# A selective-scan layer on Trainium2: gates made with the input projections and kept in DRAM, and the closing norm done in PSUM

## The chip, the cores and the metric

The kernel runs on one core of one Trainium2 chip. The metric is the device time of one execution in microseconds (us). The numbers are fp32 almost throughout, and one launch computes all four layers of the reference. The engines go by the names of the profile: PE (TensorE matmuls), PEld (its weight loads), DVE (VectorE), ACT (ScalarE), POOL (GpSimd) and SP (SyncE, which here issues the DMA transfers). Each engine takes its instructions strictly in the order in which the program lists them, and waits where an operand is not ready.

## The reference

The change lies in the first of four layers, a selective scan over 8 images of 64 channels and 64x64 pixels. Cut to what matters (L = 4096 pixels, DI = 128 inner channels, N = 16 states, K = 4 directions):

```
def _ss2d(x, ...):                                   # x: layer-normed input, B x H x W x 64
    xz = einsum('bhwc,dc->bhwd', x, in_proj_w) + in_proj_b
    xi, z = split(xz, 2, axis=-1)                    # z is the gate
    xc = silu(dwconv3(transpose(xi), conv_w, conv_b))
    xs = [xc by rows, xc by columns, both reversed]  # the 4 directions
    dts, Bs, Cs = split(einsum('bkdl,kcd->bkcl', xs, xproj_w), ...)
    dts = softplus(dtproj(dts) + dtproj_b)
    # the scan, per direction and state n:
    #   h = h * exp(dt * A) + dt * B * u ;  y += h * C
    y = sum over the directions (+ D * xs)
    y = _ln(y, outnorm_g, outnorm_b) * silu(z)       # norm and gate
    return einsum('bhwd,cd->bhwc', y, outproj_w) + outproj_b
xh = xh + _ss2d(_ln(xh, ln1_g, ln1_b), ...)
```

The other three layers (two attentions and a small trained modifier) are not touched.

## The kernel before

**Tiling and steps.** The scan layer is `scan_layer`. Channels DI lie on the 128 partitions. An image's 4096 pixels are cut into 4 chunks of 1024 (`CH`), and each of the 4 directions goes over the 4 chunks: 16 *steps* for each image, 128 in all. A step has 16 *units*, one for each state n. Below, "step 14, unit 6" means s = 14 and n = 6 of an image, both counted from 0, and images are counted from 0 to 7.

**A unit** (main loop, L991 to L1020, and `unit`, L800) has on each engine:

- ACT: `decay` (L762) makes a = exp(dt*A), issued two units ahead. For the four states in `BY_POOL` (0, 3, 6, 8), ACT copies the product that POOL made into the PSUM tile z (L777, in `spread`, at the top of the unit before). `save_state` (L798) copies one column.
- PE: for the other twelve states, PE spreads B into z (L780). Then `sum_up` (L882) adds up y = h*C over the states, in PSUM.
- DVE: z * (dt*u) (L807, twelve states) and the scan itself (L811), which gives h.
- POOL: `ct * h` (L816), and bt * (dt*u) for the four states (L770).
- SP: one load of `ct` (L758) per unit, a row of 1024 values spread to 128 partitions, 512 KB written, one unit ahead; four such loads of `bt` per step.

h and a have three buffers each, z two (PSUM), ct five.

**Background work.** Everything else is cut into *items*, a pair `(make, use)`, and put into the queue of `Background` (`bg`, L166). In each unit `bg.before` takes one item and runs its `make` (as a rule matmuls into one of two PSUM banks of 512 columns, `bank`), and at the end of the unit `bg.after` runs the `use` of the item taken the unit before (what ACT, DVE or SP do with the bank). `bg.later(f)` runs f in the same unit's `after`. The item `none` is an empty turn. In units 6, 7 and 8 (and 9 in some steps) no item with a `make` is taken. Convolutions are *groups* of up to 9 parts, at most one group a step (`credit`), which take turns with the items.

- `before(b)` (L494) makes the items for the input side of image b: load x (L507), layer norm (`norm_x`, L384: `centre` L392 to L398, `variance` L405, then a chain of small steps through DRAM for the inverse root, then `apply` L416 to L422), `project_in` (L513, L517), and eight `convolve` groups (nine matmuls L534, and Silu on ACT at L543).
- `after(b, ...)` (L564) makes the items for the output side: the squares of y (L446), `variance` (L451), the same chain, then per block of 512 pixels (eight for each image) `apply` (L470 spreads the inverse root with PE, L475 multiplies on DVE, L476 scales and shifts by on_g and on_b on ACT), `gate` (L578 projects the kept normed x with PE, L581 Silu on ACT, both issued in the same unit through `bg.later`; L589 multiplies on DVE) and `project_out` (L597, L598, L604, store L605).
- `inverse_root` (L350) holds the chain: store of the variances (L359), fetch (L366), square root on ACT (L369), reciprocal on DVE (L373), store (L374), fetch back (L378), with empty turns between.
- Silu and the square root need another function set on ACT than Exp and Ln: each of them has an ACT_TABLE_LOAD ahead of it, and `exp_and_ln` (L338) one behind it (L340).
- `pieces` (L692) splits B into three bf16 parts for a coming step: hooks at units 5, 7, 8, 9, 10 and 13 of the steps that need it. `rest(i)` puts matmuls on PE and, in the same hook, the copy of their result on ACT (L736).

**When things start.** At step 0, unit 4 of image b the items of `after(b - 1)` are queued; at step 1 of image b (step 4 of image 0) `start(b + 1)` queues those of `before(b + 1)`. In the steady images the blocks of the output side run in steps 2 to 4, the input norm in steps 5 to 7, `project_in` in 7 and 8, the convolutions from step 8 to step 0 of the next image. At the end of a unit's loop body:

```
if s == 0 and n == LAG + 2 and b > 0:
    last = images.pop(b - 1)
    bg.add(after(b - 1, last["row"], last["x"]))
    ...
if s == (1 if b else NCH) and n == 0 and b + 1 < NB:
    start(b + 1)
```

The last image's output side runs in pairs of blocks from step 13 on; the last pair comes after the scan, with nothing beside it.

Of the kernel before, what the change touches and what calls it, by code (L numbers as in the profile page):

```python
# [18 lines left out]
NB = 8  # L19
C = 64  # L20
# [224 lines left out]
def scan_layer(cm, x_in, w, xh):  # L245

    tc, nc = cm.tc, cm.nc
    with ExitStack() as ctx:
# [101 lines left out]
        def inverse_root(nb):  # L350
# [25 lines left out]
            def back(_):  # L376
                sm["r"] = work.tile([NBK, BK], F32, name="rstd", tag="rstd", bufs=1)[:nb]
                nc.sync.dma_start(sm["r"], rs.rearrange("(j f) -> j f", j=nb))  # L378

            chain = [none, (None, fetch), none, none, (None, root), (None, invert), none]  # L380
            chain += [(None, back), none, none]
            return put, chain, sm

        def norm_x(b, xn, pairs, project_in):  # L384
# [46 lines left out]
            out += chain  # L431
            out += [apply(i) for i in pairs[:2]] + [none] * (2 - len(pairs[:2]))
            for i in pairs:
                out += [project_in(2 * i), project_in(2 * i + 1)]
                if i + 2 in pairs:
                    out.insert(-1, apply(i + 2))
            return out

        def norm_y(y, blocks, load, gate, project_out):
# [25 lines left out]
            def apply(j):  # L465
# [7 lines left out]
                def use(ps):  # L473
                    v = y[:, bass.ts(j, BK)]
                    nc.vector.tensor_tensor(v, v, ps, ALU.mult)  # L475
                    nc.scalar.activation(v, v, AF.Identity, bias=on_b, scale=on_g)  # L476
# [6 lines left out]
            out += chain  # L483
            out += [apply(j) for j in blocks[:2]] + [gate(j0)]
            for j in blocks:
                if j + 2 in blocks:
                    out.append(apply(j + 2))
                out += [gate(j + 1) if j + 1 in blocks else none, project_out(j)]
            return out
# [3 lines left out]

        def before(b):  # L494

            xn = io.tile([2 * C, NBK // 2, BK], F32, name="xn", tag="xn")
# [4 lines left out]
            u = io.tile([DI, L], F32, name="u", tag="u")  # L501
            rows = BK // S
# [6 lines left out]
            def project_in(j):  # L509
# [6 lines left out]
                def use(ps):  # L516
# [3 lines left out]
                    )  # L520

# [37 lines left out]
            items = [[(None, load(j)) for j in range(NBK)]]  # L559
            for pairs in FIRST if b == 0 else (range(NBK // 2),):  # L560
                items.append(norm_x(b, xn, pairs, project_in))
            return u, block, items, [convolve(j) for j in range(NBK)]

        def after(b, y, block, blocks=range(NBK)):  # L564
# [4 lines left out]
            def load(j):  # L569
                xr = work.tile([C, BK], F32, name="xr", tag="xr", bufs=3)  # L570
                nc.sync.dma_start(xr, xf[:, bass.ts(j, BK)])
                gated[j] = xr

            def gate(j):
                def make():
                    ps = bank("zps")
# [1613 lines left out]
```

## Time and profile before

| what | number |
|---|---|
| runs | 12229.28 us median of 3 (12226.62 to 12230.54) |
| the profiled execution | 12228.28 us |
| its span, first to last instruction | 12226.5 us |
| scan layer, first to last scan instruction (L811) | 91.2 to 6913.5 us |
| start of images 1 to 7 (first scan of each) | 1002.3, 1841.4, 2681.0, 3522.7, 4364.5, 5203.5, 6053.0 us |
| DVE busy, whole span | 10380.4 us, 85% |
| ACT busy, whole span | 7575.7 us, 62% |
| POOL busy, whole span | 7247.3 us, 59% |
| PE busy, whole span | 11196.6 us, 92% |

The views used are: the page with the busy share of each engine in 40 equal slices of the span; the groups of instructions (line, engine, operation, out<-in, shapes, count, then busy us and mean ns of one, then the idle time just ahead of them and what ended most of it); the windows (busy us and number of instructions of PE, PEld, DVE, ACT and POOL in a stretch, then granted clock, DMA share and GB/s); and the timeline (start us, length, engine, line, operation, out<-in, and in brackets idle time before it and what ended that). "Idle" of an engine in a stretch is its length less the busy time. In the windows an instruction that overlaps the next is not counted twice. The scan layer fills the first 57% of the span, the first 23 slices.

### The profile page before, as it was taken

The numbers are of one execution on the slowest core, as the hardware profiler recorded it, in microseconds if no ns is written. First come the engines' busy times: TensorE is split into PE (matmuls) and PEld (weight loads), VectorE is DVE, ScalarE is ACT, GpSimd is POOL, SyncE is SP. The second block draws the span as 40 slices with busy tenths as digits, with TensorE's granted clock in tenths as the row PEclk, the third lists the DMA queues.
The fourth block names the chain that finished last, engine by engine and source line by source line (L and its number), as shares of the span: only waits on it lengthen the run. The fifth ranks groups of instructions, "written<-read, shape, count | busy, mean of one in ns | idle before, by whom it ended". The sixth has DMA issues, their size and how long they took to land. (4 is left out here: it accounts for less than half of the span.)

```text
span 12226.5 us, 120204 instructions
## 1 busy us (share of the span) xinstructions
PE 11196.6 (92%) x39087; PEld 4103.2 (34%) x39087; DVE 10380.4 (85%) x7400; ACT 7575.7 (62%) x10304; POOL 7247.3 (59%) x3326
## 2 busy tenths in 40 slices
PE   7899999999999999999998799999987779999999
PEld 2233333333333333333322233232335463333333
DVE  4999999999999999999999776868778676676767
ACT  4666667766667676676675554645547574555554
POOL 4999999999999999999999500000007480000000
PEclk8999999999999999999999899999998779999999
DMA  3666666666666666666666400000011100000000
GB/s 112 205 210 217 210 211 214 212 212 210 213 212 207 210 216 209 212 213 211 205 203 211 135 20 25 6 25 8 17 49 34 41 20 24 19 4 19 5 11 6
DMA packets 522899, 1528.62 MB, mean 125 GB/s; under 512 B 125312, under 2 KB 142352, under 8 KB 519696
## 3 DMA queue, kind: packets, MB, share of 16 engines
q1 hardware_dynamic: 522256, 1520.80, 37.9%
q8 instruction: 312, 5.11, 0.2%
q14 instruction: 331, 2.71, 0.1%
HBM read 1439.63 MB, written 72.09 MB: 124 GB/s over the span
## 5 line engine op out<-in xcount | busy, mean ns | idle before, releaser
L816 POOL TENSOR_TENSOR ct<-ct,h 128x1024 f32<-128x1024 f32 x2048 | 4789.4, 2362 | 296.8 <-DVE h L811 133.1
L882 PE MATMUL yps<-ct,lno_cen 128*128 128x512 f32 x8192 | 4119.9, 633 | 58.6 <-ACT yps L869 57.2
L811 DVE TENSOR_TENSOR_SCAN h<-a,state,z 128x1024 f32<-128x1024 f32 x1536 | 3570.4, 2341 | 82.5 <-ACT z L777 39.7
L762 ACT ACTIVATE a<-dt,amat 128x1024 f32<-128x1024 f32 x2048 | 2347.1, 1147 | 1134.8 <-DVE h L811 1128.1
L1191 DVE TENSOR_TENSOR sum<-sum,ex 128x1024 f32<-128x1024 f32 x1920 | 2347.5, 1223 | 618.5 <-ACT ex L1184 483.1
L1184 ACT ACTIVATE ex<-sc 128x1024 f32<-128x1024 f32 x2048 | 1968.0, 1024 | 1359.6 <-PE sc L1179 1359.2
L882 PEld LDWEIGHTS yps<-ct,lno_cen 128*128 128x128 f32 x8192 | 1476.4, 195 | 2078.9 <-issue 1818.0
L807 DVE TENSOR_TENSOR z<-z,e 128x1024 f32<-128x1024 f32 x1536 | 1859.8, 1211 | 128.0 <-PE z L780 75.5
L1198 PE MATMUL av<-ex,v 128*64 128x512 f32 x8192 | 1950.0, 604 | 0.0
L1179 PE MATMUL sc<-q,k 16*128 16x512 f32 (+1 forms) x8192 | 1562.1, 623 | 4.2 <-ACT q L1172 3.1
L780 PE MATMUL z<-bs,pick 48*128 48x512 bf16 x3072 | 941.9, 387 | 388.4 <-DVE h L811 339.5
L811 DVE TENSOR_TENSOR_SCAN h<-a,z 128x1024 f32<-128x1024 f32 x512 | 1161.3, 2281 | 75.0 <-ACT z L777 59.8
L770 POOL TENSOR_TENSOR bt<-bt,e 128x1024 f32<-128x1024 f32 x512 | 1209.8, 2363 | 5.4 <-DMA bt<-bc 5.4
L1505 POOL TENSOR_TENSOR gt<-gt,pad 128x1024 f32<-128x1024 f32 x16 | 34.9, 2179 | 1575.0 <-ACT gt L1504 1575.0
L1198 PEld LDWEIGHTS av<-ex,v 128*64 128x64 f32 x8192 | 512.2, 136 | 1332.7 <-issue 1278.9
L1179 PEld LDWEIGHTS sc<-q,k 16*128 16x128 f32 (+1 forms) x8192 | 528.2, 184 | 1016.4 <-issue 977.4
L777 ACT COPY z<-bt 128x1024 f32<-128x1024 f32 x512 | 519.9, 1015 | 406.0 <-DVE h L811 309.2
L780 PEld LDWEIGHTS <-pick 48*128 48x128 bf16 x3072 | 175.9, 95 | 1514.5 <-DVE h L811 931.4
L534 PE MATMUL vps<-pad,convd 128*128 128x512 f32 x1152 | 573.8, 599 | 0.1
L1878 DVE RECIPROCAL r<-e 128x512 f32<-128x512 f32 x128 | 420.6, 3322 | 0.0
L1881 POOL TENSOR_TENSOR r<-r,half 128x512 f32<-128x512 f32 x128 | 162.7, 1271 | 361.9 <-issue 186.0
L798 ACT COPY state<-h 128x1 f32<-128x1 f32 x2048 | 362.9, 177 | 0.0
(417 smaller groups left out, 9594.8 us busy)
## 6 DMA issues: line engine op xcount, KB each, us to landing
ct<-bc SPq DMA_DIRECT2D x2048, 512.0 KB
bt<-bc SPq DMA_DIRECT2D x512, 512.0 KB
x<-x SPq DMA_DIRECT2D x12, 2048.0 KB
bc<-e SPq DMA_DIRECT2D x128, 128.0 KB
x<-x SPq DMA_DIRECT2D x32, 512.0 KB
part<-x SPq DMA_DIRECT2D x128, 128.0 KB
bsd<-bp SPq DMA_DIRECT2D x192, 64.0 KB
bs<-bsd SPq DMA_DIRECT2D x128, 96.0 KB
```

The source lines that it names most:

```text
L534: nc.tensor.matmul(held[0].rearrange("p (r c) -> p r c", c=S), convd[:, t, :], pad[:, j * rows + dy : (j + 1) * rows + dy, dx : dx + S], s ...
L762: ctl["exp", n] = nc.scalar.activation(ctl["a", n], ctl["dt"], AF.Exp, scale=amat[:, ctl["k"], n : n + 1])
L770: nc.gpsimd.tensor_tensor(bt, bt, ctl["dus"], ALU.mult)
L780: nc.tensor.matmul(z[:, bass.ts(i, BK)], pick[:, n : n + 1].to_broadcast([3 * N, DI]), ctl["bs"][:, bass.ts(i, BK)], start=True, stop=True,)
L807: first = nc.vector.tensor_tensor(z, z, ctl["dus"], ALU.mult)
L811: nc.vector.tensor_tensor_scan(h[:, flip], a[:, flip], z[:, flip], 0.0 if state is None else state[:, n : n + 1], ALU.mult, ALU.add,)
L816: freed[at] = nc.gpsimd.tensor_tensor(ct, ct, h, ALU.mult)
L882: nc.tensor.matmul(ctl["ps"][:, bass.ts(i, BK)], lno_cen, ct[:, bass.ts(i, BK)], start=False, stop=(n == N - 1 and not ctl["turns"]),)
L1179: nc.tensor.matmul(sc[:, e, :], k[r : r + d, bass.ts(j, 128)], qs[i][r : r + d, :], start=True, stop=True,)
L1184: nc.scalar.activation(ex, sc, AF.Exp)
L1191: nc.vector.tensor_tensor(sums[i], sums[i], ex, ALU.add)
L1198: nc.tensor.matmul(avs[i][r, :], v[:, j, r], ex[:, e, :], start=(j == 0), stop=(j == TQ - 1))
```

## The change

- **Gates.** `gate` moves from the output side of image b to its input side: it comes behind the convolution groups of the image, its `use` is a unit after its `make`, Silu writes an SBUF tile z (three buffers), and that is stored to a DRAM tile `zd` (256 KB for each block). On the output side `load(j)` fetches it back beside x. The normed x then has one buffer in place of two.
- **Norm and gate.** ACT's scale and shift (L476) and the two DVE multiplies (L475, L589) become two DVE operations in one `use`: `ps = (y * on_g) * ps` and `z = (ps + on_b) * z`.
- **Order of the chains.** `start(b + 1)` is called at step 0, unit 4 of image b together with `after(b - 1)`. The loads of x ride on the output side's variance items, its empty turns take the input side's `centre` and `variance` items, and the turns between the output blocks take the input side's inverse-root chain. `inverse_root` gives out its four steps bare, and `spread_out` puts the empty turns between. The row of inverse roots has two buffers.
- **B's pieces.** ACT's copy of each `rest` moves to the next hook, ahead of the next matmuls or of the store.

In the order of the changed program, for image 3: loads of x in steps 0 and 1, `centre` and `variance` from step 1, unit 11 to the end of step 2, output blocks in steps 3 and 4, `apply` and `project_in` of the input in steps 4 to 6, the convolutions' Silu once a step in steps 7 to 14 (unit 0), and the eight Silus of the next image's gates in unit 4 of step 6, unit 5 of steps 11, 12 and 13, and units 4, 5, 6 and 10 of step 14. Images 1 to 6 have this pattern (image 1 has the first in unit 5). Image 0's own eight gates stand in step 4, units 3, 4, 5, 6, 10, 11, 12 and 13; four of image 1's own are left for its step 0, units 5, 6, 11 and 12.

```
 def inverse_root(nb):
-    chain = [none, (None, fetch), none, none, (None, root), (None, invert), none]
-    chain += [(None, back), none, none]
-    return put, chain, sm
+    return put, [(None, do) for do in (fetch, root, invert, back)], sm
...
+def spread_out(chain, items=()):
+    fetch, root, invert, back = chain
+    turns = [none, fetch, none, none, root, invert, none, back, none, none]
+    items = deque(items)
+    return [items.popleft() if t is none and items else t for t in turns] + list(items)
...
 def use(ps):                                   # norm_y, apply
     v = y[:, bass.ts(j, BK)]
-    nc.vector.tensor_tensor(v, v, ps, ALU.mult)
-    nc.scalar.activation(v, v, AF.Identity, bias=on_b, scale=on_g)
+    nc.vector.scalar_tensor_tensor(ps, v, on_g, ps, ALU.mult, ALU.mult)
+    multiply(j, ps)
...
-out += [apply(j) for j in blocks[:2]] + [gate(j0)]
+end = []
 for j in blocks:
-    if j + 2 in blocks:
-        out.append(apply(j + 2))
-    out += [gate(j + 1) if j + 1 in blocks else none, project_out(j)]
+    end += [apply(j), project_out(j - 1) if j - 1 in blocks else none]
+    if j % 2:
+        end.append(none)
+return out, chain, end + [project_out(blocks[-1]), none]
...
+def gate(j):                                   # now in before(b)
+    def make():
+        ps = bank("zps")
+        half, x = block(j)
+        nc.tensor.matmul(ps, win[half, 1, :], x, start=True, stop=True)
+        return ps
+    def use(ps):
+        z = work.tile([DI, BK], F32, name="z", tag="z", bufs=3)
+        nc.scalar.activation(z, ps, AF.Silu, bias=inb[:, 1:2])
+        exp_and_ln()
+        bg.later(lambda: nc.sync.dma_start(zd[:, bass.ts(j, BK)], z))
...
 def load(j):                                   # in after(b)
     nc.sync.dma_start(xr, xf[:, bass.ts(j, BK)])
-    gated[j] = xr
-def gate(j):
...
-            nc.scalar.activation(ps, ps, AF.Silu, bias=inb[:, 1:2])
...
-        nc.vector.tensor_tensor(v, ps, v, ALU.mult)
+    z = work.tile([DI, BK], F32, name="z", tag="z", bufs=3)
+    nc.sync.dma_start(z, zd[:, bass.ts(j, BK)])
+    gated[j] = (xr, z)
+def multiply(j, ps):
+    z = gated[j][1]
+    nc.vector.scalar_tensor_tensor(z, ps, on_b, z, ALU.add, ALU.mult)
...
-return [fetch, first, rest(1), rest(2), store, get]
+# middle: copy of rest(1), then the matmuls of rest(2); end: copy of rest(2), then store
+return [fetch, first, lambda: rest(1), middle, end, get]
...
+if left:                                       # start(b, left), b > 1
+    y_first, y_chain, y_end = left
+    y_first[-NBK:] = [with_load(*q) for q in zip(y_first[-NBK:], loads)]
+    bg.add(y_first + spread_out(y_chain, first))
+    chain = deque([none, *chain])
+    bg.add([chain.popleft() if t is none and chain else t for t in y_end])
+    bg.add(list(chain))
+    bg.add([(None, lambda _, b=b - 2: bg.flushed.add(b))])
...
+bg.add(end)
 bg.add([(None, lambda _: bg.groups.extend(convs))])
+bg.add(gates)
...
 if s == 0 and n == LAG + 2 and b > 0:
     last = images.pop(b - 1)
-    bg.add(after(b - 1, last["row"], last["x"]))
+    left = after(b - 1, last["row"], last["zd"])
+    if b + 1 < NB:
+        start(b + 1, left)
+    else:
+        bg.add(sequence(left))
...
-if s == (1 if b else NCH) and n == 0 and b + 1 < NB:
-    start(b + 1)
+if s == NCH and n == 0 and b == 0:
+    bg.add(later.pop(NCH))
+    start(1)
```

## The prediction

> **What bounds the kernel now.** First the page's slices: only the scan layer, slices 1 to 23, is touched, and there DVE and POOL are both at 9 tenths.
>
> ```profile
> DVE  4999999999999999999999776868778676676767
> ACT  4666667766667676676675554645547574555554
> POOL 4999999999999999999999500000007480000000
> ```
>
> ACT is at 6 or 7 there: it has room on average, and matters only where it is late. Next the groups of DVE in the six middle images (1002 to 6053 us).
>
> ```profile
> L811 DVE TENSOR_TENSOR_SCAN h<-a,state,z 128x1024 f32<-128x1024 f32 x1153 | 2680.0, 2341 | 50.6 <-ACT z L777 18.5
> L807 DVE TENSOR_TENSOR z<-z,e 128x1024 f32<-128x1024 f32 x1152 | 1394.4, 1210 | 47.0 <-PE z L780 23.7 <-ACT u L543 5.0 <-ACT e L639 4.7
> L811 DVE TENSOR_TENSOR_SCAN h<-a,z 128x1024 f32<-128x1024 f32 x384 | 870.9, 2281 | 23.2 <-ACT z L777 12.4 <-POOL ct L816 0.6
> L589 DVE TENSOR_TENSOR y<-zps,y 128x512 f32<-128x512 f32 x48 | 32.1, 670 | 6.2 <-ACT zps L581 5.8
> L475 DVE TENSOR_TENSOR y<-y,rps 128x512 f32<-128x512 f32 x48 | 31.7, 661 | 0.0
> ```
>
> The idle columns add to 127 us of 5051: DVE sets the pace, and no reordering can win more than this there. Third, the windows, one step of image 3 each: steps 3, 4, 7, 10 and 14.
>
> ```profile
> 2839.80:2897.60 57.80, 55.23 (x125) 17.39 (x124) 54.96 (x36) 44.28 (x63) 50.79 (x22) 1.00 0.60 197
> 2897.60:2951.60 54.00, 48.09 (x108) 15.63 (x108) 51.65 (x32) 36.26 (x52) 50.54 (x22) 0.97 0.68 216
> 3055.70:3112.60 56.90, 55.15 (x119) 18.43 (x119) 52.14 (x31) 38.48 (x60) 51.34 (x23) 0.88 0.58 190
> 3214.30:3265.30 51.00, 50.28 (x125) 18.14 (x123) 50.57 (x30) 35.93 (x55) 51.00 (x23) 1.00 0.65 222
> 3418.30:3471.70 53.40, 49.51 (x112) 17.98 (x112) 50.70 (x30) 35.02 (x50) 51.36 (x23) 0.94 0.57 200
> ```
>
> Length less the third busy time is DVE's idle: 2.84, 2.35, 4.76, 0.43 and 2.70 us. The quiet step 10 shows the floor, 0.43. Over the floor, the six images lose 34.7 us in steps 3 and 4, 13.5 in step 7, 5.9 in step 14. Fourth, why: the timeline of ACT, and of DVE (last line), in step 3.
>
> ```profile
> 2857.58 1.28 ACT L581 ACT_TABLE_LOAD   x1 [4.16 <-PE zps L578]
> 2858.88 0.66 ACT L581 ACTIVATE zps<-zps,inb 128x512 f32<-128x512 f32 x1
> 2859.56 1.28 ACT L340 ACT_TABLE_LOAD   x1
> 2860.85 0.81 ACT L476 ACTIVATE y<-y,on_b,on_g 128x512 f32<-128x512 f32 x1
> 2861.57 1.00 ACT L777 COPY z<-bt 128x1024 f32<-128x1024 f32 x1
> 2862.68 2.35 DVE L811 TENSOR_TENSOR_SCAN h<-a,state,z 128x1024 f32<-128x1024 f32 x1 [2.42 <-ACT z L777]
> ```
>
> The gate's Silu is issued in the same unit as its matmul, so ACT stands 4.16 us behind PE, then needs 3.23 us (1.28+0.66+1.28) for Silu with two table loads and 0.81 for L476. The copy of z for unit 6 stands behind all that, and the scan waits 2.42 us for it.
>
> **The change part by part.** The sum is made against the profiled execution's 12228.3 us (span 12226.5), 1.0 below the median.
>
> *A. Gates leave steps 2 to 4; L476 goes.* No Silu and no 0.81 us copy stand ahead of z there; what stays (xo of L604, dt and e) is in quiet steps too. Of 34.7 us I take 33 away. Bounds: half of it (17), all (35).
>
> *B. The input norm leaves step 7* for steps 4 to 6, which have neither the 2 us copy L681 nor `lower` items. ACT still waits for DVE at L422, but hand-adding its rows from the end of unit 5's multiply (L422 0.81, pad 0.68, decay and state 1.22, e 1.05, z 1.0: 4.8 us) leaves it ahead of the 5.8 us that DVE takes to unit 8's scan. Of 13.5 us, 12 goes. Bounds 0 and 13.5.
>
> *C. Image 6* runs two convolutions a step now, and its steps 11 to 14 idle 10.8 us, where images 1 to 5 idle 3.9 on average. The convolutions come a step or more sooner and no longer double: 7 goes. Bounds 0 and 7.
>
> *D. Image 7 and the tail.* The same waits (L589 and z) take 7.9 us in its steps; 8 goes. After the scan, from the first L475 (6935.2) to the last output (6949.7), the chain multiply, L476, Silu, multiply becomes two multiplies a block: second pair done about 6938.4, and the last pair of matmuls (2 times 1.96, slow clock) ends at 6942.3: 7 goes. D is 15; bounds 7 and 17.
>
> *E. DVE's own work.* 64 blocks had 0.661 + 0.670 us. The nearest rows for a multiply with a column operand:
>
> ```profile
> L2130 DVE SCALAR_TENSOR_TENSOR x<-yps,gp,x 128x512 f32<-128x512 f32 x32 | 24.0, 750 | 83.4 <-PE yps L1762 83.4
> L1872 DVE SCALAR_TENSOR_TENSOR half<-htps,at 128x512 f32<-128x512 f32 x128 | 80.7, 672 | 23.6 <-ACT at L1865 18.4 <-POOL t L1883 3.2 <-POOL t L1882 1.0
> ```
>
> L2130 has a column (gp), L1872 a constant. I take 750: 64 x (1.500 - 1.331) = +10.8 us, all on DVE. Lower bound, by 672: +0.8. [...]
>
> *F. The gates in step 14.* Three Silus come in units 4, 5, 6. Today's ACT in that step:
>
> ```profile
> 3433.84 0.19 ACT L798 COPY state<-h 128x1 f32<-128x1 f32 x1
> 3433.92 1.02 ACT L777 COPY z<-bt 128x1024 f32<-128x1024 f32 x1
> 3438.11 1.05 ACT L664 ACTIVATE e<-e 128x1024 f32<-128x1024 f32 x1
> ```
>
> It has no idle time from 3415.0 up to that copy (Silu of the convolution, L681, dt, e, the copies of y). The scan of unit 6 starts at 3436.80. With 3.23 us ahead of it the copy ends at 3438.17: 1.4 us late. Behind it come decay and state 1.17, gate 3.23, decay and state 1.22, gate 3.23, e 0.96, and z for unit 8 0.95: 10.8 us, where DVE is back in 5.8 us (3.50 + 2.26 between scan starts). 5.0 us late. Together 6.3 us, x6 images = 38, less the 5.9 us of idle there now, which it swallows: +32. Bounds: 0, if ACT catches up, and 6 x 9.7 us (three gates in full) = 58. [...] The single gates in unit 5: the same rows end z for unit 8 at 3442.6, when its scan is due at 3442.55, so 0. In unit 4 of step 6 (3018.4 to 3021.8) ACT has 1.0 us idle and the copy 2.3 us of slack: 0.
>
> *G. Image 0, step 4* has four Silus in a row in units 3 to 6 (by the same adding 6.3 us, 2 of them idle now: +5), *image 1, step 0* two (units 5 and 6: z ends at 1029.4, its scan was at 1026.6: +3). Together +8; bounds 0 and 20.
>
> *At nothing.* Stores and fetches of z, 64 each of 256 KB: 34 MB beside 1500, at a DMA share of 0.57 to 0.70. Three fetches of z with x and xr follow each other in step 0, 0.4 MB more than the queues move in three units at their present rate over share; ct's one unit of lead hides the 1.2 us (uncovered: 7 us over six images). On SP the store of z waits for Silu, with the next ct loads behind it: by the times of F they go at 3437, 3443 and 3447, POOL wants them at 3444 and after. The loads of x pass from step 4 to steps 0 and 1; their one buffer was last read in step 14. In the pieces of B, ACT no longer stands behind PE (165.9 us in 120 waits at L736), but no scan waits for it; PE's second `rest` now stands behind ACT's copy, covered by z and the sum in unit 9, 2 us; uncovered 60 x 0.37 = 22 us.
>
> Sum: -33 -12 -7 -15 +10.8 +32 +8 = -16. Predicted: 12212 us.
>
> **The rivals.** A difference under 0.2%, 24.5 us, can't be told from none: 12205 to 12254 is "same".
>
> *1. ACT hides the bunches.* For it: 62% busy, and a single gate finds its 3.23 us. Against: it has no idle in units 0 to 5 of step 14. F falls to 0 and G to 5: -51, 12177.
>
> *2. The gates cost their full length: slower.* PE stands behind ACT: there are two banks, the third gate's matmul waits for the first Silu, and z for the next units is behind it on PE (L780 is already DVE's largest releaser, 23.7 us). Then step 14 costs 9.7 us, and the four single gates the 1.84 us that a gate in step 4 cost now: 6 x 17 = 102, image 0 and 1 20. -67 + 10.8 + 122 = +66, 12294. Stalls at gates of 56 us use up A to E; from 81 us on the kernel is slower by over 0.2%. Against: the matmul of the third gate is due after 3437, when the first Silu has ended.
>
> *3. The output blocks' waits move along*, and A and B return half: +7 on balance, 12235; that stays "same".
>
> **How the numbers follow.** The forecast, with rival 3, has 0.46 (own range 12190 to 12240), rival 1 0.30, rival 2 0.24. Faster: 0.29 of rival 1 and 0.12 of the forecast's lower end, 0.41. Slower: 0.22 of rival 2. Same: 0.37. The range 12160 to 12270 leaves out a quarter of rival 1 (0.08) and half of rival 2 (0.12).
>
> **What would show it.** Windows of steps 3, 4 and 7: DVE idle under 1 us (A, B). Groups: the two new operations at 750 ns (E). Step 14: waits for z by ACT in units 6 and 8, 1.4 and 5 us (F). The tail some 7 us shorter (D). If steps 11 to 13 idle by over 1.5 us each at unit 8, or PE's z ends DVE's waits in step 14, rival 2 is right. Wrong in kind would be POOL as the new bound: it is 51.0 of 51.0 us busy in step 10, and 816 of an image's 842.

## The result, and the profile after

The changed kernel takes 12280.65 us (median of 5, 12274.97 to 12288.27) where the kernel before takes 12229.28 in the same session: a ratio of 1.0042, 95% interval 1.0031 to 1.0053. The prediction was 12212 us, 16 us less than before, with a range of 12160 to 12270; the kernel came out 51 us slower. A later pair of the same two kernels on another chip gave 1.0036 (1.0022 to 1.0049). The kernel before reads between 12217 and 12229 us from chip to chip, so below kernels are compared by their ratio to it.

The page of the changed kernel looks as before: DVE and POOL full in the scan layer, ACT at 6 or 7 tenths.

```profile
DVE  4999999999999999999999876868778676676767
ACT  4676676776766766766666454646547574555554
POOL 4999999999999999999999700000006480000000
```

DVE's groups over images 1 to 6 (1010 to 6117 us: 5107.6 us, where the kernel before needed 5050.8). The columns are xcount | busy, mean ns of one | idle before, and what ended it.

```profile
L832 DVE TENSOR_TENSOR_SCAN h<-a,state,z 128x1024 f32<-128x1024 f32 x1152 | 2679.1, 2342 | 81.0 <-ACT z L798 40.5 <-POOL ct L837 9.2 <-issue 0.2
L828 DVE TENSOR_TENSOR z<-z,e 128x1024 f32<-128x1024 f32 x1152 | 1394.3, 1210 | 71.5 <-PE z L801 37.4 <-POOL ct L837 12.7 <-PE xps L521 6.7
L832 DVE TENSOR_TENSOR_SCAN h<-a,z 128x1024 f32<-128x1024 f32 x384 | 871.2, 2281 | 16.4 <-ACT z L798 4.3 <-POOL ct L837 2.1
L604 DVE SCALAR_TENSOR_TENSOR z<-rps,on_b,z 128x512 f32<-128x512 f32 x48 | 36.1, 751 | 1.7
L479 DVE SCALAR_TENSOR_TENSOR rps<-y,on_g,rps 128x512 f32<-128x512 f32 x48 | 35.1, 730 | 0.0
```

The scans and products cost what they did. The idle column went from 127 us to 171: +44 of the +57 us. ACT's z ends 45 us of it (31 before) and PE's z 37 (24 before). The rest, 13 us, is DVE's own work.

Where the idle time lies shows in the windows: from:to, length, busy of PE, PEld, DVE, ACT and POOL, the granted clock of PE, the DMA share and GB/s. Steps 0, 1, 3, 4, 5, 7, 10, 13 and 14 of image 3, changed kernel:

```profile
2713.40:2764.50 51.10, 50.62 (x119) 16.18 (x119) 49.85 (x29) 36.00 (x59) 50.22 (x23) 0.97 0.77 235
2764.50:2816.40 51.90, 48.25 (x118) 16.32 (x117) 50.81 (x30) 36.79 (x61) 51.18 (x23) 1.00 0.78 244
2869.70:2926.50 56.80, 52.20 (x119) 16.39 (x117) 56.23 (x38) 32.75 (x49) 50.54 (x22) 1.00 0.64 218
2926.50:2981.10 54.60, 51.03 (x114) 16.22 (x114) 54.08 (x36) 30.33 (x46) 50.66 (x22) 0.97 0.65 217
2981.10:3040.80 59.70, 58.46 (x116) 19.19 (x116) 53.47 (x34) 37.26 (x56) 51.56 (x23) 0.83 0.52 173
3093.10:3144.20 51.10, 49.81 (x123) 18.21 (x123) 50.67 (x30) 36.79 (x55) 51.10 (x23) 1.00 0.69 222
3248.30:3299.30 51.00, 50.28 (x125) 18.14 (x123) 50.57 (x29) 36.04 (x55) 51.00 (x23) 1.00 0.68 222
3401.70:3456.70 55.00, 52.22 (x114) 18.41 (x114) 50.76 (x29) 37.69 (x53) 50.53 (x23) 0.91 0.59 196
3456.70:3515.30 58.60, 46.34 (x102) 15.50 (x102) 50.92 (x29) 47.33 (x61) 52.68 (x23) 0.94 0.60 203
```

Length less DVE's busy time: steps 3 and 4 idle 0.57 and 0.52 us (2.84 and 2.35 before), step 7 0.43 (4.76 before). But step 5 idles 6.23 us with the clock at 0.83, step 13 4.24 at 0.91, and step 14 7.68. In the kernel before, steps 5 and 13 of this image idle 0.75 and 1.02 us:

```profile
2951.60:3003.30 51.70, 49.17 (x110) 16.28 (x110) 50.95 (x30) 35.75 (x56) 50.99 (x23) 0.93 0.64 212
3366.50:3418.30 51.80, 48.09 (x112) 17.51 (x112) 50.78 (x29) 34.95 (x50) 51.61 (x23) 0.97 0.62 203
```

Summed over images 1 to 6 from the trace, DVE's idle time by step, and PE's time at half clock in the last column (us):

```
kernel       s0-1  s2-4  s5-6    s7  s8-12   s13   s14   s15    sum   half clock
before        6.8  48.7   8.9  16.1   22.9  11.5   8.3   3.8  126.9    277
changed      23.8  18.3  24.1   2.6   24.7  24.0  44.6   8.9  170.9    365
changed, 2nd 25.7  19.8  18.5   2.6   27.3  21.2  44.1   8.6  167.7    345
```

The second row of the changed kernel says how well one profile repeats: within 3 us in most columns, 6 in steps 5 and 6.

Step 14 first, as the prediction had it. ACT's timeline from unit 5 on, then DVE's:

```profile
3471.85 1.14 ACT L783 ACTIVATE a<-dt,amat 128x1024 f32<-128x1024 f32 x1
3472.89 0.18 ACT L819 COPY state<-h 128x1 f32<-128x1 f32 x1
3473.09 1.28 ACT L541 ACT_TABLE_LOAD   x1
3474.38 0.69 ACT L541 ACTIVATE z<-zps,inb 128x512 f32<-128x512 f32 x1
3475.09 1.28 ACT L340 ACT_TABLE_LOAD   x1
3476.38 1.02 ACT L798 COPY z<-bt 128x1024 f32<-128x1024 f32 x1
```

```profile
3477.50 2.35 DVE L832 TENSOR_TENSOR_SCAN h<-a,state,z 128x1024 f32<-128x1024 f32 x1 [2.20 <-ACT z L798]
3479.83 1.23 DVE L828 TENSOR_TENSOR z<-z,e 128x1024 f32<-128x1024 f32 x1
3481.10 2.35 DVE L832 TENSOR_TENSOR_SCAN h<-a,state,z 128x1024 f32<-128x1024 f32 x1
3488.49 2.35 DVE L832 TENSOR_TENSOR_SCAN h<-a,state,z 128x1024 f32<-128x1024 f32 x1 [5.05 <-ACT z L798]
```

Three gates of 3.25 us stand in ACT's queue (the first is shown), the copy of z for unit 6 behind the first and that for unit 8 behind the third. The scans wait 2.20 and 5.05 us; the prediction had 1.4 and 5.0.

Step 13 has one gate only, with its Silu in unit 5, and DVE's product for unit 7 still waits 3.79 us:

```profile
3426.27 1.23 DVE L828 TENSOR_TENSOR z<-z,e 128x1024 f32<-128x1024 f32 x1 [3.79 <-ACT z L798]
```

The profile puts this wait down to ACT's copy of z, but that copy is the one for unit 8, and that it ends just before the product is chance. In all six images this product starts 0.20 to 0.21 us behind the end of PE's spread of z for unit 7, whichever engine the profile names. So PE's own timeline tells why (in square brackets, the idle time before an instruction and what ended it; "x4" is four records, two to an fp32 matmul: L536 has 128 for the 64 gates):

```profile
3411.05 0.60 PE L801 MATMUL z<-bs,pick 48*128 48x512 bf16 x2 [0.85 <-DVE h L832]
3411.58 1.13 PE L557 MATMUL vps<-pad,convd 128*128 128x512 f32 x2
3413.26 0.59 PE L887 MATMUL yps<-nil 1*128 1x512 bf16 x2 [0.55 <-ACT y L867]
3413.78 0.65 PE L801 MATMUL z<-bs,pick 48*128 48x512 bf16 x2
3415.29 3.75 PE L903 MATMUL yps<-ct,lno_cen 128*128 128x512 f32 x4 [0.86 <-ACT yps L890]
3418.97 2.07 PE L536 MATMUL zps<-xn,win 64*128 64x512 f32 x2
3420.97 3.70 PE L903 MATMUL yps<-ct,lno_cen 128*128 128x512 f32 x4
3424.50 1.02 PE L557 MATMUL vps<-pad,convd 128*128 128x512 f32 x2
3425.46 0.60 PE L801 MATMUL z<-bs,pick 48*128 48x512 bf16 x2
```

PE stands idle three times, 2.26 us within 6 us. From 3414.2 to 3424.5 the granted clock is 0.5, and a group of four records takes 3.7 us (1.96 at full clock, in e10 below). In that stretch the gate's matmul costs 2.07 us, and z for unit 7, behind it, comes at 3425.5.

### The profile page after: what moved, and what is told of

Read it like the earlier page. It is cut to its first block, busy times and chain, and to the rows that moved or that the text cites. A ratio compares the mean times of both kernels' runs of the same rounds, so it can differ in the third digit from the quotient of the medians.

```text
span 12279.4 us, 120472 instructions
## 1 busy us (share of the span) xinstructions
PE 11244.5 (92%) x39087; PEld 4116.2 (34%) x39087; DVE 10393.6 (85%) x7400; ACT 7540.9 (61%) x10240; POOL 7247.2 (59%) x3326
## 5 line engine op out<-in xcount | busy, mean ns | idle before, releaser
L819 ACT COPY state<-h 128x1 f32<-128x1 f32 x2048 | 361.9, 177 | 10.5 <-DVE h L832 10.5
```

## The experiments

Theory 1: gates in ACT's queue cost steps 13 and 14. Theory 2: the loads moved to steps 0 and 1 delay ct. Theory 3: the interleaved norms give nothing. Theory 4, formed after the first runs: PE's clock makes step 13. The diffs are against the changed kernel unless another is named. The table at the end of the section has the idle time of each run.

**e1_plain_gate: the gate without Silu and without its table loads.**

```
-                    nc.scalar.activation(z, ps, AF.Silu, bias=inb[:, 1:2])
-                    exp_and_ln()
+                    nc.scalar.activation(z, ps, AF.Identity, bias=inb[:, 1:2])
```

> Leaves out the Silu on the gate: the copy of the gate out of PSUM stays on ScalarE, at the same place and with the same store, but as Identity with the bias (an operation that this kernel has elsewhere), and the table load after it goes with it. Theory 1 (the changed kernel lost its time where gates stand in ScalarE's queue with two table loads of 1.28 us each, 2.57 us of 3.25 us per gate): steps 13 and 14 of images 1 to 6 together lose 40 of their 69 us of VectorE idle, step 6 and 15 some 5, and the kernel takes about 12230 us (-50; 12220 to 12245). Rival (the time went to the added transfers and the place of the other moves, and ScalarE has room for the gates): within 12 us of the changed kernel's 12281, with step 14's waits still there. If PE's slow stretches follow from ScalarE being late, the time at the halved clock (365 us over images 1 to 6) falls towards the 277 of before; if they come of the order of matmuls itself, it stays above 340.

12242.98 against 12218.74: 1.0013 (1.0004 to 1.0023): some 28 to 35 us less than the changed kernel, where 50 were expected. Step 14's idle fell from 44.6 to 20.5 us, but step 13's did not fall at all (26.1), and the half clock rose to 416 us. In step 14 no scan waits for ACT's z any more (40.1 us in the changed kernel); what is left is mostly the product of unit 7, 17.6 us, in all six images 0.2 us behind PE's z. Step 13's window is that of the changed kernel almost to the digit, with 2.4 us less on ACT, and its wait is there too, where ACT's copy (L797) has ended 1.3 us before:

```profile
3384.90:3439.90 55.00, 52.25 (x114) 18.42 (x114) 50.81 (x29) 35.30 (x51) 50.75 (x23) 0.91 0.60 197
3409.48 1.23 DVE L827 TENSOR_TENSOR z<-z,e 128x1024 f32<-128x1024 f32 x1 [3.73 <-POOL ct L836]
```

So ACT's time is not what step 13 waits for. Theory 1 holds for step 14 alone, and even there PE is late behind ACT.

**e2_gate_a_step: the same work, one gate per step, in unit 10.**

```
-                bg.add(gates)
+                bg.add([(None, lambda _: ready.extend(gates))])
...
+                        if n == 9 and ready:
+                            bg.add([ready.popleft()], first=True)
```

> The whole work of the changed kernel, with another order: each of the eight gates of images 1 to 7 is made in the second half of a step of its own (unit 10, steps 7 to 15 as the convolutions finish) in place of units 4 and 5 and of three at once in step 14. Theory 1 (a bunch of gates is what ScalarE can't take up before VectorE's state is due; one gate per step costs at most the 1 us that steps 11 and 12 show): step 14 falls from 44.6 us of idle in images 1 to 6 to about 10, step 13 from 24 to about 13, the other steps gain up to 1 us each per image, in sum -30 to -45, 12236 to 12251. Rival (every gate costs its share of 3.25 us on ScalarE wherever it stands, so the order does not matter): within 10 us of 12281, with the idle of step 14 spread over steps 7 to 15.

12225.72 against 12218.74: 1.0006 (0.9996 to 1.0016), 37 to 44 us less than the changed kernel by the difference of the ratios. Step 14 idles 3.1 us and step 13 12.6 (8.3 and 11.5 before the change). By the trace the gates now stand in steps 6 to 13, one each. Steps 8 to 13 idle 39.5 us, where those of the kernel before, without gates, idle 34.4: the gates themselves cost little; where they stood cost 53 us (41.5 in step 14, 11.4 in step 13). DVE's idle time in all fell by 42 only, as steps 0 and 1 idle 9 us more than in the changed kernel; no run says why.

**e3_no_columns: plain products in place of the two with a column.** Left out are the norm's scale and shift.

```
-                    nc.vector.scalar_tensor_tensor(ps, v, on_g, ps, ALU.mult, ALU.mult)
+                    nc.vector.tensor_tensor(ps, v, ps, ALU.mult)
...
-                nc.vector.scalar_tensor_tensor(z, ps, on_b, z, ALU.add, ALU.mult)
+                nc.vector.tensor_tensor(z, ps, z, ALU.mult)
```

> Leaves out the norm's scale and shift (here ones and zeros): plain products in place of the two scalar_tensor_tensor operations, everything else as in the changed kernel. It prices the column operand. If the two operations with a column take what their rows show (731 and 751 ns) against 661 to 670 for a plain product of that size, 48 blocks in images 1 to 6 and 16 more give 64 x 0.15 = 9.7 us: 12271 (12264 to 12278). If the column operand is free and the rows hold only the wait between the two operations, the time stays within 3 us of 12281.

12255.88 against 12218.74: 1.0028 (1.0018 to 1.0038), 10 to 17 us less than the changed kernel by the difference of the ratios; the intervals overlap, so this is not clear of noise by itself. The rows are 674 and 692 ns in place of 731 and 751, so the column costs 58 ns an operation, 64 x 0.116 = 7.4 us. The other 35 ns of a block stay with plain products (674 and 692 against 661 and 670 before). The first now writes to PSUM and the second reads what the first has just written; which of the two costs it is not shown.

**e4_fetch_later: the first three fetches of z and the stored rows with the last three variance items.**

```
-                    if j - j0 < 3:
+                    if nb < 8 and j - j0 < 3:
                         load(j)
+                    if nb == 8 and j >= 5:
+                        load(j - 5)
```

> The first three fetches of z and of the stored rows are issued with the last three variance items and not with the first three, behind the loads of x that the change moved to steps 0 and 1; nothing else. Theory 2 (steps 0 and 1 lost 17 us over images 1 to 6, their VectorE idle 6.8 to 23.8 us, because POOL's ct waits for a transfer that stands behind the loads of x and these fetches): idle of steps 0 and 1 falls to 6 to 14 us and the kernel takes 12266 to 12276. Rival (the loads of x alone, or the input norm's own work, take that time): within 4 us of 12281 with the idle unchanged. A third way: the fetches are late for steps 2 to 4, whose DVE idle (18 us) grows, and the time goes above 12290.

12264.10 against 12218.74: 1.0037 (1.0023 to 1.0052), 0 to 6 us less: not to be told from none by itself. The profile is plainer: step 1 idles 4.8 us (13.5 before the edit), step 0 still 10.3. In step 1 of the changed kernel 10.7 us of DVE's waits are put down to POOL's product with ct, with this edit 2.2. POOL's product with ct, the one that was waited for, in the kernel before, the changed one and this one:

```profile
L816 POOL TENSOR_TENSOR ct<-ct,h 128x1024 f32<-128x1024 f32 x1537 | 3594.3, 2363 | 151.6 <-DVE h L811 57.3 <-DMA ct<-bc 51.0 <-PE rps L470 11.6
```

```profile
L837 POOL TENSOR_TENSOR ct<-ct,h 128x1024 f32<-128x1024 f32 x1537 | 3591.7, 2357 | 208.4 <-DMA ct<-bc 94.1 <-DVE h L832 79.7 <-PE yps L903 12.9
```

```profile
L839 POOL TENSOR_TENSOR ct<-ct,h 128x1024 f32<-128x1024 f32 x1537 | 3594.2, 2361 | 192.3 <-DMA ct<-bc 84.5 <-DVE h L834 74.3 <-PE yps L905 16.8
```

Waiting for ct's transfer grew by 43 us with the change; this edit takes 10 of them back. Theory 2 is right for step 1; no run moves the loads of x alone. Step 0 lost 7 us for other reasons: one wait of 3.6 us in image 1, at unit 8 for ACT's z, behind the two gates that the prediction's G counts there (it is gone in e5, where no gate stands alone), and some 0.8 us in each of images 2 to 6, in units 2 and 4, which no run explains. On top of one gate per step the same edit gave more:

**e6_step_and_later: e2 and e4 together (the two diffs above).**

> Two edits together: one gate per step made in unit 10 (as in the run that gave 12225.72), and the first three fetches of z and the stored rows with the last three variance items. If the two causes are separate, the gain of the second in step 1 (8.7 us of VectorE idle over images 1 to 6, and some 10 over all) adds to the first: step 1 at about 6 us of idle, step 13 and 14 as there, 12213 to 12220 where before reads 12218.7, a ratio of 0.9995 to 1.0002. If they are not (ScalarE and PE in steps 0 and 1 are what is late), it stays at 12222 to 12230.

12210.03 against 12217.60: 0.9992 (0.9983 to 1.0001). Step 1 went from 17.2 us of idle (e2) to 7.7; in this step the two causes add up.

**e5_one_table: the gate's Silu right behind the convolution's, under the same table; its matmul follows the convolution's last.**

```
                 def use(ps):
                     nc.scalar.activation(u[:, bass.ts(j, BK)], held[0], AF.Silu, bias=convb)
-                    exp_and_ln()
                     if b:
+                        z = work.tile([DI, BK], F32, name="z", tag="z", bufs=3)
+                        nc.scalar.activation(z, ps, AF.Silu, bias=inb[:, 1:2])
+                        bg.later(lambda: nc.sync.dma_start(zd[:, bass.ts(j, BK)], z))
                         bg.done[b] += 1
+                    exp_and_ln()
...
+                    count -= b > 0
...
+                    if b:
+                        return items + [(gate(j)[0], use)]
...
-                bg.add(gates)
```

> The whole work of the changed kernel; for images 1 to 7 gate j's matmul follows convolution j's last part, and its Silu runs right behind the convolution's, under the same table: no gate has table loads of its own (16 per image fewer, 16 x 1.28 = 20.5 us of ScalarE), and no gate stands in unit 5 or in a bunch in step 14. Theory 1 (bunches with their own table loads): step 14 of images 1 to 6 falls from 44.6 us of idle to under 12, step 13 from 24 to under 14; the conv's turn on ScalarE is 0.7 us longer, up to 0.5 us per step in unit 7 or 8; 12215 to 12240 where before reads 12229. Rival (each gate costs wherever it is): above 12260. A third way: two Silus and two table loads in one turn are 4.0 us in a row, which puts new waits of over 1 us into steps 7 to 14, 12240 to 12260.

12210.42 against 12217.60: 0.9997 (0.9987 to 1.0006). Steps 13 and 14 idle 3.8 and 5.7 us, less than in the kernel before; step 7 takes back 10.

**e7_table_and_later: e5 and e4 together (their two diffs).**

> The gate's Silu right behind the convolution's under one table load, with the fetches moved to the last three variance items. Theory: it is the run with the one table less about 10 us (step 1 from about 13 us of idle to about 5 over images 1 to 6). If ScalarE's freed 20 us per image are what steps 0, 5, 6 and 13 wanted, it lies below the run with one gate per step and the same fetches, at 12200 to 12212 where before reads 12218.7; if those steps wait for the order of matmuls and not for ScalarE's time, it lies within 5 us of that run.

12193.58 against 12217.60: 0.9983 (0.9974 to 0.9992), faster than the kernel before and 16 us below e6 on the same chip. The gain over e6 lies beyond steps 13 and 14: steps 0 and 1 idle 11.0 us against e6's 23.8. Whether ACT's saving (16 table loads an image) or the gates' other place makes it, no run takes apart.

**e8_norms_apart, e9_table_later_apart, e13_apart_alone: the interleaving undone, on e6, on e7, and on the changed kernel alone.** The same edit in all three:

```
-                    bg.add(y_first + spread_out(y_chain, first))
-                    chain = deque([none, *chain])
-                    bg.add([chain.popleft() if t is none and chain else t for t in y_end])
-                    bg.add(list(chain))
+                    bg.add(sequence((y_first, y_chain, y_end)))
                     bg.add([(None, lambda _, b=b - 2: bg.flushed.add(b))])
+                    bg.add(first + spread_out(chain))
```

> The kernel with one gate per step and the later fetches, with the interleaving undone: image b+1's input norm is queued behind image b-1's output norm and not between its items (its loads of x stay with the variance items). It tests the prediction's term of -12 us for the input norm that leaves step 7. Theory 3 (the input norm costs what it costs wherever its rps and projections stand; the 13.5 us won in step 7 came back in steps 5 and 6): idle of steps 5 and 6 falls from about 21 us over images 1 to 6 to about 9, step 7 rises from 5 to about 16, and the kernel is within 5 us of the interleaved one. Rival (the interleaving is worth its 12 us, and steps 5 and 6 were hurt by the gates): slower by 8 to 15 us. A third way: with the convolutions later again, gates and convolutions share steps 8 to 15 more tightly, and steps 13 to 15 lose over 10 us.

> Three edits on the changed kernel: gate's Silu behind the convolution's under one table load, the later first fetches, and image b+1's input norm queued behind image b-1's output norm. If the interleaving costs some 10 us wherever it stands (12210 with it, 12200 without it in the kernels with one gate per step), this one takes 12180 to 12190 where before reads 12217.6. If the 10 us came of the place that the gates had in those kernels, it stays at 12190 to 12200.

> The changed kernel with one edit: image b+1's input norm is queued behind image b-1's output norm and not between its items; gates, fetches and loads stay as they are. It isolates the term of -12 us that the prediction gave the interleaving. Theory 3 (the interleaving won its 12 us in step 7 and gave back at least as much in steps 5, 6 and 15, by the clock that PE loses there): the kernel is 5 to 15 us faster than the changed one, a ratio of 1.0025 to 1.0033, step 7's idle back at 10 to 16 us over images 1 to 6 and that of steps 4 to 6 lower by as much or more. Rival (the interleaving is worth 12 us where gates are made in units 4 and 5 and in step 14): 8 to 15 us slower, 1.0045 to 1.0055.

e8: 12199.97, 0.9988 (0.9979 to 0.9997), 10 us below e6 on the same chip. e9: 12183.67 against 12217.07, 0.9973 (0.9962 to 0.9983), the fastest of all, against 0.9983 with the interleaving. e13: 12256.78 against 12218.43, 1.0033 (1.0020 to 1.0045), against 1.0042 and 1.0036. No single pair of intervals is apart, but all three lean the same way: the interleaving shows no gain, and by the medians it costs some 4 to 12 us. The steps answered only in part as expected: in e13 steps 5 and 6 fell to 11.2 us (8.9 in the kernel before), step 7 rose to 7.2 and not to 10 or more, and the late gates moved idle time from step 14 (24.6) to step 15 (31.3). In e8, whose gain of 10 us neither theory 3 nor its rival foretold, step 7 rose by 4.6 and steps 5 and 6 fell by 2.7 only; the gain is spread over many steps.

**e10_keep_busy: a matmul more.** The first matmul of each convolution is made twice.

```
-                        for t in range(t0, t1):
+                        again = t0 == 0 and b > 0
+                        for i, t in enumerate([0] * again + list(range(t0, t1))):
...
-                                start=(t == 0), stop=(t == 8),
+                                start=(t == 0), stop=(t == 8 or (again and i == 0)),
```

> Adds work and changes nothing else: in images 1 to 7 the first matmul of each convolution is made twice into the same bank (8 per image, 0.86 us each at full clock), in step 13 in unit 4 ahead of the sum's first matmuls, where PE stands idle for 0.55 us behind ScalarE. Theory 4 (in step 13 the gate costs because PE's idle time in units 3 to 5 halves its clock, and the gate's matmul then stands at 2.0 us and not 0.86 in front of z of unit 7): with that idle time filled the clock stays full, time at the half clock in step 13 falls from 58 us over images 1 to 6 to under 35 and VectorE's idle there from 24 to 5 to 14 us; step 14 keeps its 40 to 45 us; the kernel is 5 to 15 us faster than the changed one, a ratio to before of 1.003 or less. Rival (ScalarE's lateness and the matmuls' own time, with the clock only a sign of it): 0.86 us more PE work in front of z(7), idle of step 13 grows to 26 to 29 us and the kernel is up to 5 us slower, a ratio of 1.0042 to 1.0046.

12254.43 against 12217.07: 1.0029 (1.0019 to 1.0040). With more work on PE the kernel is faster by 9 to 16 us in the medians, by the difference of the ratios; the intervals overlap, so for the whole kernel this is not clear of noise by itself. Step 13 is plain: its idle went from 24.0 us (21.2 in the second profile) to 4.0, its half clock from 58 us to 0, and step 14 kept its 43.0. PE's timeline in step 13, the same place as above:

```profile
3400.13 0.60 PE L802 MATMUL z<-bs,pick 48*128 48x512 bf16 x2 [0.85 <-DVE h L833]
3400.67 1.99 PE L558 MATMUL vps<-pad,convd 128*128 128x512 f32 x4
3402.58 0.60 PE L888 MATMUL yps<-nil 1*128 1x512 bf16 x2
3403.12 0.60 PE L802 MATMUL z<-bs,pick 48*128 48x512 bf16 x2
3404.44 1.96 PE L904 MATMUL yps<-ct,lno_cen 128*128 128x512 f32 x4 [0.72 <-ACT yps L891]
3406.33 1.12 PE L536 MATMUL zps<-xn,win 64*128 64x512 f32 x2
3407.38 1.98 PE L904 MATMUL yps<-ct,lno_cen 128*128 128x512 f32 x4
3409.20 1.02 PE L558 MATMUL vps<-pad,convd 128*128 128x512 f32 x2
3410.15 0.60 PE L802 MATMUL z<-bs,pick 48*128 48x512 bf16 x2
```

The doubled matmul (x4 for x2) fills the 0.55 us in front of the sum's first matmuls. The two other gaps are still there, but the clock holds: the gate's matmul takes 1.1 us and not 2.07, a group of four 1.96 and not 3.75, and z for unit 7 comes 10.0 us after z for unit 4, not 14.4. The two groups of four and the gate's matmul account for these 4.4 us. Theory 4 is right for step 13, its rival (idle up to 26 to 29 us) wrong. Part of the gain is lost elsewhere: steps 5 to 7 idle 41.7 us, where the changed kernel's two profiles have 26.7 and 21.1; no run says why.

**e11_three_ops: norm and gate as three operations, on e9.**

```
-                    nc.vector.scalar_tensor_tensor(ps, v, on_g, ps, ALU.mult, ALU.mult)
-                    multiply(j, ps)
+                    nc.vector.tensor_tensor(v, v, ps, ALU.mult)
+                    nc.scalar.activation(v, v, AF.Identity, bias=on_b, scale=on_g)
+                    if j - 1 in blocks:
+                        multiply(j - 1, y[:, bass.ts(j - 1, BK)])
...
-                nc.vector.scalar_tensor_tensor(z, ps, on_b, z, ALU.add, ALU.mult)
+                nc.vector.tensor_tensor(z, ps, z, ALU.mult)
```

> On the kernel with one table, later fetches and the norms apart (12183.67, a ratio of 0.9973): the norm and gate are again three operations, a plain product on VectorE (661 ns before), scale and shift on ScalarE (0.8 us), and a plain product with the fetched gate, issued behind the next block's first product. It tests the prediction's term of +10.8 us for the two operations with a column. If the column operands cost what their rows say (731 and 751 against 661 and 670 ns, 151 ns a block), VectorE's busy time falls by 9 to 11 us and the kernel takes 12170 to 12178 where before reads 12217. Rival (64 more operations of 0.8 us on ScalarE in steps 2 to 4, next to the chain of the state, cost as much as they save): within 4 us of 12184, or above it, with the idle of steps 2 to 4 up from 15.5 us over images 1 to 6.

12430.53 against 12219.94: 1.0168 (1.0154 to 1.0182). This experiment misses its aim. An item's matmul is issued before the operations of the item ahead of it, so the projection reads the gate before its product: the product with y is left out of what is projected, and each product waits for that matmul (120.2 us in the row). It says nothing of the prediction's term E. But its row holds a number of its own:

```profile
L616 DVE TENSOR_TENSOR z<-y,z 128x512 f32<-128x512 f32 x64 | 106.4, 1663 | 133.6 <-PE ops L623 120.2 <-issue 6.9 <-ACT y L482 4.2
```

Shortest, median and longest of the 64 are 665, 1562 and 4911 ns, where the products of the same size with an operand in PSUM took 660 to 693 ns (L475 and L589, before).

**e12_after_again: the changed kernel, unedited.**

> The changed kernel itself, unedited, beside the run above and the kernel before on one chip: it gives the size that the differences are taken from. All theories expect the ratio of 1.0042 again, within its interval (1.0031 to 1.0053); a ratio outside would mean that the differences between runs of different calls, taken through the kernel before, are off by that much.

12266.79 against 12219.94: 1.0036 (1.0022 to 1.0049), inside the first interval.

DVE's idle time by step over images 1 to 6, and PE's at half clock, for all that bear on it (us):

```
kernel   s0-1  s2-4  s5-6    s7  s8-12   s13   s14   s15    sum  half clock  ratio
e1       23.5  22.6  16.5   3.8   30.0  26.1  20.5  11.7  154.6     416     1.0013
e2       33.2  19.7  21.6   5.3   26.9  12.6   3.1   6.5  128.8     332     1.0006
e3       23.5  25.2  18.6   4.4  30.8  22.7  43.3   8.5  177.0     410     1.0028
e4       15.1  21.6  18.1   3.3   23.4  20.6  43.2   9.1  154.3     362     1.0037
e10      24.0  13.1  30.4  11.3   20.6   4.0  43.0   7.3  153.7     277     1.0029
e13      24.8  17.1  11.2   7.2   19.7  13.8  24.6  31.3  149.6     317     1.0033
e6       23.8  17.9  16.8   8.0   28.2  11.5   2.7   6.4  115.4     287     0.9992
e8       20.9  16.8  14.1  12.6   22.6  10.7   5.6   3.1  106.4     277     0.9988
e5       19.1  23.9  25.8  12.9   22.0   3.8   5.7   7.9  120.9     304     0.9997
e7       11.0  16.3  19.2   9.7   21.9   3.8   4.7   4.4   91.0     222     0.9983
e9       15.3  15.5   7.4  11.8   20.5   3.8   3.5   4.4   82.1     198     0.9973
```

The fastest, e9, keeps the gates made ahead and the norm in PSUM, and undoes the rest of what the runs took apart: the interleaving, the gates' own table loads and places, and the early fetches. The early start with the loads of x and the change to B's pieces are still in it; no run takes these two apart. Its scans wait for ACT's z 1.2 us in six images, where the changed kernel waits 40.5:

```profile
L840 DVE TENSOR_TENSOR_SCAN h<-a,state,z 128x1024 f32<-128x1024 f32 x1153 | 2679.7, 2341 | 34.5 <-POOL ct L845 2.0 <-ACT z L806 1.2
```

## Why the prediction was wrong

The forecast was -16 us against the profiled run, and the result +53 (12281.14 against 12228.28). Three steps of the prediction failed, each a cost that it put at nothing: B's new place for the input norm, F's single gates in unit 5, and the loads and fetches in steps 0 and 1. One by one:

- **A (gates leave steps 2 to 4, -33): right.** Idle 48.7 to 18.3, -30.4, of which 26.9 lie in steps 3 and 4, where the prediction had read its 34.7.
- **B (input norm leaves step 7, -12): the first step that failed.** Step 7's idle did fall by 13.5 us, but that of steps 5 and 6, where the work went, rose by 15.2 (9.6 in the second profile). The prediction costed the new place at 0 by adding up ACT's rows alone; in step 5 it is PE that is late, at a clock of 0.83, with the norm's spread and projection (L414, L521) in its queue. With the interleaving undone three kernels were faster in the medians, and in e13 steps 5 and 6 are back at 11.2 us.
- **C (image 6, -7): right, as far as it can be told.** In steps 11 to 14 image 6 idles 12.0 us, and images 1 to 5 now idle 13.3 there, so its excess of 7 us is gone. Image 6 went from 849.5 to 854.0 us, +4.5, while images 1 to 5 went up by 10.5 on the mean: some 6 us in its favour.
- **D (image 7 -8, tail -7): half.** From the last scan to the scan layer's last output the kernel is 5.2 us shorter (34.5 to 29.3 us); image 7 gained 1.7 us and not 8 (862.8 to 861.1). In all, the time behind the last scan fell by 9.8 us (5313.0 to 5303.2), but 4.5 of them lie in the three layers that the change does not touch, and no run shows a reason.
- **E (DVE's own work, +10.8): right.** By the rows 64 x (731 + 751 - 661 - 670) ns = 9.7 us; DVE's busy time on the page rose by 13.2. By e3 the column itself makes 7.4 us of it.
- **F (three gates in step 14, +32): right in mechanism and size.** Idle +36.3, at units 6 and 8, waiting for ACT's z. What e1 leaves there shows that PE is late too, hidden behind ACT. **F's clause "The single gates in unit 5 ... so 0" is the second step that failed.** It followed ACT's queue only, by the rows of step 14, and e1 shows that ACT's time is not what counts in step 13. The gate's matmul also stands in PE's queue in front of z for unit 7, and PE had just lost half its clock there: step 13 lost 12.5 us, and e10 shows the clock as the cause (24.0 to 4.0 us with more work on PE). The gates of steps 11 and 12 stand at 17 and 7 us of half clock over the six images, where step 13 has 58, and steps 8 to 12 cost 2 us together: a single gate costs little where PE's clock holds.
- **G (image 0 +5, image 1's step 0 +3): about right.** Image 0 took 7.2 us more, and image 1's step 0 waits 3.6 us at unit 8.
- **"At nothing", the third step that failed:** steps 0 and 1 lost 17.0 us, of which G had foretold 3. The prediction named the uncovered price of the fetches, 7 us, and said ct's lead hides it. It does not: waiting for ct's transfer grew by 43 us on POOL, and e4 and e6 take back 9 us of idle in step 1 by moving fetches. Of step 0's 7 us about half is G's wait in image 1, and the rest is not explained by any run. Step 15's +5 was not foretold either.

Of the 69 us between forecast and result, three misses of 12 to 14 us make 40: B with its new place (+1.7 for -12), steps 0 and 1 (+17.0 for +3) and step 13 (+12.5 for 0). The rest is in small terms: step 15, image 7, F, A and E each a few us worse than their price, and C's 7 us, which the figures of the steps contain already. Rival 2's number (12294) came nearest, but by luck: it has 102 us for the gates of images 1 to 6, and steps 13 and 14 lost 49. Its sign, PE's z ending DVE's waits in step 14, did not come (ACT's z ends 40 of the 45 us there); PE's z ended them in step 13. Its mechanism, every gate at full length, is wrong: in e2 the 36 gates of steps 8 to 13 cost 5 us at most.

e5 and e7, where the gate's Silu runs under the table load of the convolution's, lie 0.0009 below e2 and e6 in their ratios, some 11 us. The gates stand elsewhere in them too, so the saving by itself is not shown.

## What to carry to other kernels

Work that is moved is costed in every queue in which it stands. A matmul that comes to stand in front of a due one is priced at the clock that PE will have there: the gate's took 2.07 us where PE had just been waiting, and 1.12 where the clock held. Three gates in a bunch found no slack here, where the same gates, one to a step, cost little. And a gain read from one step's idle time is only a gain when the step that receives the work has been costed by the same views.

## What the hardware showed

**PE's clock fell after short waits.** The clock record of the changed kernel is in stretches that are, but for one, multiples of 3.41 us, at 1 or 0.5. Set against PE's idle time in the stretch of 3.41 us before (scan layer, 2017 stretches):

```
PE idle in a stretch at full clock   stretches   next one at half clock
under 0.35 us                          1438           0
0.35 to 0.70                            129           4
0.70 to 1.05                            176          23
1.05 to 1.40                             39          16
over 1.40                                68          56
```

Back at half clock, 98 of 132 stretches with under 0.35 us of idle return to full clock, and 2 of 35 with more. The kernel before gives the same picture, with 2 of 1446 in the first row and 55 of 74 in the last. So a microsecond of idle time in a stretch was often followed by the half clock (16 of 39 stretches with 1.05 to 1.40 us). In 33 of 35 cases it then stayed until PE had worked a stretch through, and one such stretch was not always enough (34 of 132 were followed by another at half clock). In step 13 three gaps of 0.55 to 0.86 us, 2.26 in sum, came just ahead of the fall.

**A product of two SBUF operands on DVE** took 665 to 4911 ns in e11, beside a POOL that is 8 or 9 tenths busy in the scan layer; with one operand in PSUM it took 660 to 693 (L475 and L589, before). In e11's trace 20 of the 64 products start while POOL is idle and take 665 to 694 ns. Each of the other 44 ends 0.55 us behind the end of a POOL instruction, however long it has run until then. The kernel before and the changed one both keep one operand of the norm's and the gate's products in PSUM.
